# A greedy planner for a four-layer graph network gets a rank and a lead for every kind of operation

## The chip, the core and the metric

The kernel runs on one core of a Trainium2 chip. The metric is the device time of one execution in microseconds (us): the median of several runs. The core has five engines with a queue of instructions each. TensorE (PE) multiplies matrices, and its weight loads (PEld) overlap with its products. VectorE (DVE) and ScalarE (ACT) do elementwise work, GpSimd (POOL) here only the small powers of -0.5, and SyncE (SP) issues all transfers. Each queue is worked off in the order in which the program has written it; semaphores make one engine wait for another.

## The reference

64 graphs of 256 nodes with 256 features pass through four layers in float32. Each layer is `x = layernorm(x + f(x, adj))`:

- Layer 0: four heads; `q`, `k` and `X` are leaky-ReLU projections, `att = sigmoid(q k^T / 8) * adj`, scaled on both sides by the root of the degrees, times `X`, then a layer norm with gain and bias.
- Layer 1: attention with eight heads of 32, masked where `adj` is 0, softmax, times `v`, output projection.
- Layer 2: `adj @ x + eps * x`, a 256 to 1024 projection, RMS norm, SiLU, a 1024 to 256 projection.
- Layer 3: graph attention: `e = leaky(s1_i + s2_j)`, masked softmax, times `x W`, layer norm, exact GELU.

```python
A = dis[..., :, None] * adj_h * dis[..., None, :]          # layer 0
attn = jax.nn.softmax(jnp.where(adj > 0, scores, NEG))     # layer 1, eight heads
h = jax.nn.silu(_rmsnorm(agg @ W1 + b1, rms_weight))       # layer 2
h_prime = jnp.matmul(jax.nn.softmax(e_masked, axis=2), Wh) # layer 3
```

## The kernel before

`weights` describes the loads and small preparations of the constants, and `graph`, called once for each of the 64 graphs, describes the four layers of one graph. Neither issues anything: each call of `op` makes an `Op` with an engine, a planned cost in ns, a function that will issue its instructions, and the values that it reads and writes. A value is a tile of one of six kinds: `s` (128x512, SBUF, 42 slots), `d` (128x1024, 10), `b` (128x2048, 3), `c` (128x32, 72), `p` (a PSUM bank, 8) and `h` (scratch in HBM, 8). The dependencies come from readers and writers.

`Plan.order` then makes the order of all queues by a greedy simulation. It keeps a clock for each engine, and again and again it looks at all operations whose predecessors are placed. For each it works out the earliest start from the engine's clock, the time when its inputs have landed and the time when enough slots are free, and it places the one with the smallest key:

```python
key = start, op.due, op.graph, op.index
```

`due` (lines 149 to 152) runs backwards from the results: it is the least `due` of the successors, held down by the operation's own `turn`. A turn is a number, four to a graph, and stands for one activation table (sigmoid, exp, SiLU, GELU in this order); the turns are opened one after the other (lines 213 to 216), so that ScalarE loads each table once a turn, and at any time several graphs are under way, each in another layer (`ROUND`). Operations without predecessors, which are loads, may be placed when their `due` is within `AHEAD` turns of the open one. `TAIL`, `NEAR` and `ENDS` change a few steps for the first and the last graphs, where a transposition goes over TensorE and not over HBM, or an elementwise step over ScalarE and not VectorE.

TensorE has modes. Most products use the full array. Lines 502 and 582 (scores of layers 0 and 1) run several small products side by side in tiles of rows ("rows"); lines 520, 542, 618 and 680 (degree sums, `A @ X`, attention times `v`, mean of squares) do so in tiles of columns ("columns"). Transposes are a mode of their own. `CHANGE` holds what a switch of mode costs. Because switching costs, the planner adds `STAY` to the start of every TensorE operation of another mode while it is in rows or columns:

```python
if op.engine == "PE" and mode in ("rows", "columns") and mode != op.mode:
    start += STAY - 60 * (op.mode == "transpose")
```

`join` (lines 103 to 143) welds the mean of squares of one graph (line 678) to the first half of layer 1's scores of a graph three further on (line 578), for most graphs; the pair counts as one operation from then on. `emit` sorts the operations by planned start and calls their functions, and that is the order of the instructions in every queue. Slots are given out by the planner too, so waits on buffers follow from the plan.

The names that come up below: line 368 is every product that gives features by tokens (`w_q`, `w_k`), 379 every one that gives tokens by features; 649 is `adj @ x`, 661 the wide projection of layer 2, 707 the narrow one, 722 the projection of layer 3; 323, 625, 693 and 731 are transposes. 470 is the exponential of both softmaxes, 465 the masking in front of it, 697 and 699 the scaling and the SiLU of layer 2, 406, 528 and 688 the powers on GpSimd.

Of the kernel before, what the change touches and what calls it, by code (L numbers as in the profile page):

```python
# [27 lines left out]
DMA_KB, DMA_SEEN = 4, 1900  # L28

WORDS = {"s": 516, "d": 1024, "b": 2048, "c": 32, "p": 512, "h": 1024}  # L30
AHEAD = 12
STAY = 200
NEAR = 1, 2, 3

ENDS = 3
# [3 lines left out]
ROUND = 0, 2, 5, 7  # L39
TAIL = 0, 1, 3, 4  # L40
SLOTS = {"s": 42, "d": 10, "b": 3, "c": 72, "p": 8, "h": 8}


class Value:
# [3 lines left out]
    def __init__(self, kind, name, parts=1):  # L48
        self.kind, self.name = kind, name
        self.writer, self.readers = [None] * parts, [[] for _ in range(parts)]  # L50
        self.uses, self.slot, self.end, self.t = 0, None, 0.0, None
        if kind == "const":
            self.uses, self.slot = 1 << 30, -1
# [29 lines left out]
class Plan:  # L83
# [4 lines left out]
    def __init__(self, graphs):  # L88
        self.graphs = graphs
        self.ops, self.turns = [], {}  # L90
        self.graph = 0

    def op(self, engine, cost, fn, w=(), r=(), turn=None, mode="full", after=None, size=0, joint=None):

        pair = lambda x: (x[0], None if x[0].kind == "p" else x[1]) if isinstance(x, tuple) else (x, None)
        w, r = [pair(x) for x in w], [pair(x) for x in r]
        op = Op(engine, cost, fn, w, r, self.graph, turn, mode, after, size)
        op.table, op.joint, op.leaves = turn is not None and engine == "ACT", joint, mode
        if op.table:
            self.turns[turn] = self.turns.get(turn, 0) + 1  # L100
        self.ops.append(op)

    def join(self):

        joints, before = {}, {}
        for op in self.ops:
            if op.joint is not None:
                joints.setdefault(op.joint[0], []).append(op)
            for nxt in op.after:
                before.setdefault(nxt, []).append(op)  # L110
        gone = set()
        for ops in joints.values():
            if len(ops) == 1:
                continue
            ops.sort(key=lambda op: op.joint[1])
            one, fns = ops[0], [op.fn for op in ops]
            prior = list(dict.fromkeys(p for op in ops for p in before.get(op, ())))
            assert not set(prior) & set(ops)
            for p in prior:
                p.after = list(dict.fromkeys(one if nxt in ops else nxt for nxt in p.after))  # L120
            one.after = list(dict.fromkeys(nxt for op in ops for nxt in op.after))
            for nxt in one.after:
                before[nxt] = list(dict.fromkeys(one if p in ops else p for p in before[nxt]))
                nxt.waits = len(before[nxt])
            before[one], one.waits = prior, len(prior)
            one.fn = lambda fns=fns: [fn() for fn in fns]
            one.cost = sum(op.cost for op in ops) + sum(CHANGE[a.mode, b.mode] for a, b in zip(ops, ops[1:]))
            one.leaves = ops[-1].mode
            one.turn = max((op.turn for op in ops if op.turn is not None), default=None)
            values = [v for op in ops for v in op.values]  # L130
            one.values = list(dict.fromkeys(values))
            for v in one.values:
                v.uses -= values.count(v) - 1
            gone.update(ops[1:])
# [10 lines left out]
    def order(self):  # L145
        for i, op in enumerate(self.ops):
            op.index = i
        self.join()
        for op in reversed(self.ops):
            op.due = min((nxt.due for nxt in op.after), default=4 * (min(op.graph + ROUND[3], self.graphs - 1 + TAIL[3]) + 1))  # L150
            if op.turn is not None:
                op.due = min(op.due, op.turn)
        clock = {e: 0.0 for e in AFTER}
        self.free = {k: [(0.0, i) for i in range(n)] for k, n in SLOTS.items()}
        turns, left = sorted(self.turns), dict(self.turns)
        turn, loaded, mode, moved = 0, None, "full", 0.0
        ready = {op for op in self.ops if not op.waits}
        done = []
        self.busy = {e: 0.0 for e in AFTER}
        while ready:  # L160
            best = None
            for op in ready:
                if (op.due - AHEAD if op.first else op.turn or 0) > turns[turn]:
                    continue
                start = clock[op.engine]
                if op.engine == "PE" and mode in ("rows", "columns") and mode != op.mode:
                    start += STAY - 60 * (op.mode == "transpose")
                start = max(start, op.ready)
                need = {}
                for v in op.values:  # L170
                    if v.slot is None:
                        need[v.kind] = need.get(v.kind, 0) + 1
                for kind, n in need.items():
                    free = self.free[kind]
                    if len(free) < n:
                        break
                    start = max(start, sorted(free)[n - 1][0])
                else:
                    key = start, op.due, op.graph, op.index
                    if best is None or key < best[0]:  # L180
                        best = key, start, op
            if best is None:
                raise RuntimeError(f"the plan is stuck at {len(done)} of {len(self.ops)}")
            _, start, op = best
            op.start = start
            ready.discard(op)
            if op.table and op.turn != loaded:
                op.start, loaded = op.start + TABLE_LOAD, op.turn
            if op.engine == "PE":
                op.start = max(op.start, clock["PE"] + CHANGE.get((mode, op.mode), 0))  # L190
                mode = op.leaves
            end = clock[op.engine] = op.start + op.cost
            op.landed = end + op.seen
            if op.engine == "SP":
                moved = max(moved, end) + op.size * DMA_KB
                op.landed = max(op.landed, moved + DMA_SEEN)
            self.busy[op.engine] += op.cost
            done.append(op)
            op.takes = [v for v in op.values if v.slot is None]
            for v in op.takes:  # L200
                self.free[v.kind].sort()
                v.slot = self.free[v.kind].pop(0)[1]
            for v in op.values:
                v.uses -= 1
                v.end = max(v.end, op.landed)
                if not v.uses:
                    self.free[v.kind].append((v.end, v.slot))
            for nxt in op.after:
                nxt.waits -= 1
                nxt.ready = max(nxt.ready, end + ITSELF[op.engine] if nxt.engine == op.engine != "SP" else op.landed)  # L210
                if not nxt.waits:
                    ready.add(nxt)
            if op.table:
                left[op.turn] -= 1
                while turn < len(turns) - 1 and not left[turns[turn]]:
                    turn += 1
        assert len(done) == len(self.ops)
        self.span = max(op.start + op.cost for op in done)
        return sorted(done, key=lambda op: op.start)
# [533 lines left out]
def gnn_stack_kernel(ctx: ExitStack, tc: tile.TileContext, t: dict, out: bass.AP):  # L753
# [20 lines left out]
        {"space": {"p": bass.MemoryType.PSUM, "h": bass.MemoryType.DRAM}[kind]} if kind in "ph" else {})))  # L774
        for kind in SLOTS}

# [60 lines left out]
```

## Time and profile before

| | |
|---|---|
| median of 3 runs | 2696.62 us (2696.18 to 2699.69) |
| the profiled execution, span | 2698.6 us |
| instructions | 56499 |
| TensorE busy | 2666.0 us, 99% |
| weight loads busy | 2144.9 us, 79% |
| VectorE busy | 2436.7 us, 90% |
| ScalarE busy | 2228.8 us, 83% |
| GpSimd busy | 588.5 us, 22% |
| DMA | 501.01 MB, mean 186 GB/s; the one queue that moves data 67.0% of 16 engines |

The profile is one execution; its span, from the first instruction to the last, is 2.0 us above the median. A busy share is a mean over the whole span. TensorE's products are pipelined and the ends of its instructions are modelled, so the distance from one start to the next says more than the busy time does. In a line of the timeline stand the start, the length in us, the engine, the line of the program, the operation, what is written and read, the shape and the number of instructions; a bracket at the end names what ended an idle time before it. "PE ps L722 <- DVE hT L697: 0.6, 2, 0.4" reads: TensorE at line 722 waited for VectorE's line 697, 0.6 us in all, 2 times, 0.4 at the most.

### The profile page before, as it was taken

What the parts mean: (1) busy time and instruction counts of PE and PEld (TensorE: products, weight loads), DVE (VectorE), ACT (ScalarE), POOL (GpSimd) and SP (SyncE); (2) the same over time, 40 slices, a digit from 0 to 9 for tenths busy, and PEclk for the clock granted to TensorE, in tenths of its full rate; (3) what the DMA queues carried; (4) which work ended last, traced back from release to release, by engine and by line L of the source; (5) the groups of instructions that cost most, each with busy time, mean ns of one, the idle gap of its engine ahead of it and who ended that gap; (6) DMA issues with size and microseconds to landing.
All of it is one profiled execution on the core that took longest, in us unless ns stands there. A gap on an engine that the chain in (4) does not pass through costs nothing.

```text
span 2698.6 us, 56499 instructions
## 1 busy us (share of the span) xinstructions
PE 2666.0 (99%) x17568; PEld 2144.9 (79%) x17568; DVE 2436.7 (90%) x7480; ACT 2228.8 (83%) x5343; POOL 588.5 (22%) x902
## 2 busy tenths in 40 slices
PE   8999999999999999999999999999999999999997
PEld 6777788887887878878888878888788788787776
DVE  6789999999899999999999999989999899999986
ACT  4888888888888988888888888888888888888886
POOL 1111222212222212222222222222222222222212
PEclk9999999999999999999999999999999999999999
DMA  4476875766767767667767677677676676776661
GB/s 146 133 213 176 219 219 161 211 192 183 200 185 187 215 178 189 196 181 207 202 169 206 186 190 212 173 190 201 172 213 193 169 212 189 186 212 181 169 173 36
DMA packets 708045, 501.01 MB, mean 186 GB/s; under 512 B 309792, under 2 KB 667552, under 8 KB 707744
## 3 DMA queue, kind: packets, MB, share of 16 engines
q1 hardware_dynamic: 707744, 497.40, 67.0%
q8 instruction: 140, 2.29, 0.4%
q14 instruction: 161, 1.32, 0.2%
HBM read 301.35 MB, written 195.82 MB: 184 GB/s over the span
## 4 chain that ended last, share of the span: by engine, by line
PE 93%; DVE 3%; ACT 2%; DMA 1%; SPq 1%; issue 1%; POOL 0%; ACTq 0%; POOLq 0%; DVEq 0%
PE ps L368 16%; PE ps L707 16%; PE ps L661 16%; PE ps L379 15%; PE ps L582 5%; PE ps L502 4%; PE ps L542 4%; PE av L618 4%; PE ps L722 4%; PE ps L649 4%; PE ps L323 1%; PE ps L520 1%; PE pr L693 1%; DVE e L465 1%; PE ps L731 0%
## 5 line engine op out<-in xcount | busy, mean ns | idle before, releaser
L470 ACT ACTIVATE e<-e,low 128x256 f32<-128x256 f32 x1152 | 574.6, 500 | 83.7 <-DVE low L465 82.9
L707 PE MATMUL ps<-w,hT 128*128 128x256 f32 x2048 | 466.8, 380 | 1.3 <-ACT hT L699 1.2
L661 PE MATMUL ps<-aggT,w 128*128 128x256 f32 x2048 | 463.4, 380 | 1.6 <-ACT aggT L359 1.0
L707 PEld LDWEIGHTS ps<-w,hT 128*128 128x128 f32 x2048 | 385.7, 190 | 60.4 <-issue 4.6
L661 PEld LDWEIGHTS ps<-aggT,w 128*128 128x128 f32 x2048 | 383.3, 190 | 57.0 <-issue 2.8
L405 POOL TENSOR_SCALAR mv<-mv 128x2 f32<-128x2 f32 x384 | 127.8, 333 | 1316.8 <-DVE mv L395 888.0
L465 DVE CUSTOM_DVE_ANT_0 e<-ps,adj 128x256 f32<-128x256 f32 x1024 | 361.7, 418 | 30.0 <-PE ps L582 29.9
L406 POOL TENSOR_TENSOR mv<-mv,mhalf 128x2 f32<-128x2 f32 x384 | 306.0, 797 | 32.0
L603 DVE STREAM_TRANSPOSE eb<-e 128x1024 f32<-128x1024 f32 x248 | 300.8, 1221 | 0.8 <-ACT e L470 0.7
L668 ACT ACTIVATE hT<-ps,br,r 128x256 f32<-128x256 f32 x512 | 255.7, 585 | 33.9 <-PE ps L707 30.6
L393 DVE BATCH_NORM_STATS2 st<-y 128x6 f32<-128x256 f32 x640 | 238.3, 408 | 1.2
L420 ACT ACTIVATE x<-y,mv 128x256 f32<-128x256 f32 x384 | 215.2, 600 | 28.9 <-DVE mv L416 26.1
L666 ACT ACTIVATE sq<-ps,b 128x256 f32<-128x256 f32 x512 | 220.0, 474 | 20.2 <-PE ps L661 19.7
L470 ACT ACTIVATION_READ_ACCUMULATOR e<-e,low 128x1 f32 x1152 | 219.0, 190 | 0.0
L508 DVE TENSOR_TENSOR att<-att,adjT 128x512 f32<-128x512 f32 x256 | 166.4, 676 | 10.0 <-ACT att L506 10.0
L688 POOL TENSOR_TENSOR rs<-rs,mhalf 128x2 f32<-128x2 f32 x64 | 45.6, 712 | 540.4 <-DVE rs L686 518.9
L528 POOL TENSOR_TENSOR dp<-dp,mhalf 128x8 f32<-128x8 f32 x64 | 110.2, 1722 | 215.8 <-DVE dp L527 168.3
L697 DVE TENSOR_TENSOR hT<-hT,pr 128x1024 f32<-128x1024 f32 x128 | 150.0, 1210 | 5.2 <-PE pr L693 4.3
L582 PE MATMUL ps<-kT,qT 32*128 32x256 f32 x2048 | 146.2, 399 | 0.0
L673 DVE TENSOR_TENSOR sq<-sq 128x512 f32<-128x512 f32 x192 | 129.5, 675 | 11.1 <-ACT sq L666 10.2
L368 PE MATMUL ps<-x0T,w_q 128*128 128x256 f32 x512 | 130.4, 385 | 6.6 <-DMA x0T<-in_xT 6.6
L506 ACT ACTIVATE att<-ps 128x512 f32<-128x512 f32 x256 | 132.2, 603 | 3.8 <-PE ps L502 3.1
(119 smaller groups left out, 5508.9 us busy)
## 6 DMA issues: line engine op xcount, KB each, us to landing
far<-eb SPq DMA_DIRECT2D x248, 512.0 KB, 3.6
eT<-far SPq DMA_DIRECT2D x992, 128.0 KB, 4.1
adj<-in_adj SPq DMA_DIRECT2D x128, 256.0 KB, 5.1
far<-eb SPq DMA_DIRECT2D x488, 64.0 KB, 2.0
x0T<-in_xT SPq DMA_DIRECT2D x64, 256.0 KB, 4.7
adjT<-in_adjT SPq DMA_DIRECT2D x64, 256.0 KB, 4.9
x<-in_x SPq DMA_DIRECT2D x64, 256.0 KB, 5.2
adj<-in_adjT SPq DMA_DIRECT2D x64, 256.0 KB, 4.8
```

Source lines behind the costliest of these rows:

```text
L368: pe.matmul(two(ps)[:, o, :], w.t[:, k, o * P:(o + 1) * P], two(xT)[:, k, :], start=(k == 0), stop=(k == DB - 1))
L379: pe.matmul(two(ps)[:, n, :], two(xT)[:, k, n * P:(n + 1) * P], w()[:, k, :], start=(k == 0), stop=(k == DB - 1))
L393: op("DVE", 328, lambda n=n: dve.bn_stats(st.t[:, 6 * n:6 * n + 6], two(src)[:, n, :]), [(st, n)], [(src, n)])
L406: pool.tensor_tensor(m()[:, :, 2], m()[:, :, 2], c.mhalf[:, :NB], OP.pow)
L465: op("DVE", 345, lambda n=n: dve.tensor_tensor_reduce(out=E(n), in0=two(logits)[:, n, :], in1=two(negmask)[:, n, :], scale=-scale, scalar= ...
L470: op("ACT", 491, lambda n=n: act.activation(E(n), E(n), AF.Exp, bias=low.t[:, n:n + 1], scale=-1.0, accum_out=r.t[:, col(n):col(n) + 1]), ...
L582: pe.matmul(two(pss[i])[:, n, :], two(qT1)[s, hq, n * P:(n + 1) * P], two(kT1)[s, hq, :], start=True, stop=True)
L603: op("DVE", 1155, lambda e=e, eb=eb: dve.transpose(eb.t.rearrange("p (b g i) -> p g b i", b=4, i=32), e.t.rearrange("p (g b i) -> p g b i" ...
L661: pe.matmul(two(ps)[:, i, :], c.w2_1.t[:, k, (j + i) * P:(j + i + 1) * P], two(aggT)[:, k, :], start=(k == 0), stop=(k == DB - 1))
L666: op("ACT", 357, lambda ps=ps, sq=sq, i=i, j=j: act.activation(two(sq)[:, i, :], two(ps)[:, i, :], AF.Square, bias=c.b2_1.t[:, j + i:j + i ...
L668: op("ACT", 491, lambda ps=ps, i=i, j=j: act.activation(Hb(j + i)[:, 0], two(ps)[:, i, :], AF.Identity, bias=c.br2.t[:, j + i:j + i + 1], ...
L707: pe.matmul(two(ps)[:, n, :], Hb(j)[:, 0, n * P:(n + 1) * P], c.w2_2.t[:, j, :], start=(j == 0), stop=(j == HB - 1))
```

## The change

The operations stay as they are, with their costs, values and engines. Every operation gets a kind: the place in the program where it was described, the engine, and its how-manieth it is of these in its graph. All 64 graphs share their kinds; there are 323 in all. `RANK` and `LEAD` hold a number for each kind. `RANK` is added to `due` and `LEAD` (in ns) to the start in the planner's key; the start at which an operation is then placed is the unchanged one. The lead is thus a preference between candidates; the planned start still follows from the clock, the inputs and the slots. Three constants change beside this.

```diff
-AHEAD = 12
-STAY = 200
+AHEAD = 13
+STAY, TURN_STAY = 157, 40
...
+RANK = [
+    0.68, 2.14, 0.01, 0, -0.77, 0.92, -6.01, -4.32, -4.54, -14.31, 2.22, -2.5, 0.34, 0, -4.24, -0.65, -2.92,
...
+LEAD = [
+    0, 0, 0, 0, 33, 209, 0, 98, 689, -8, 30, -381, -441, 197, -191, 0, -61, 0, 3, -17, 0, -27, 457, 0, 15, 37,
...
     def __init__(self, graphs):
         self.graphs = graphs
         self.ops, self.turns = [], {}
+        self.seen = {}
...
         self.ops.append(op)
+        kind = fn.__code__.co_firstlineno, engine
+        n = self.seen.get((self.graph, kind), 0)
+        self.seen[self.graph, kind] = n + 1
+        op.kind = kind, n
...
+        ranks = {}
+        for op in self.ops:
+            op.rank = ranks.setdefault(op.kind, len(ranks))
...
-                    start += STAY - 60 * (op.mode == "transpose")
+                    start += STAY - TURN_STAY * (op.mode == "transpose")
...
-                    key = start, op.due, op.graph, op.index
+                    key = start + LEAD[op.rank], op.due + RANK[op.rank], op.graph, op.index
```

Of the 323 ranks 213 are not zero: 32 of 53 kinds on TensorE, 68 of 107 on VectorE, 47 of 75 on ScalarE, all 8 on GpSimd, 58 of 80 on SP. Of the leads 79 are not zero: 9 on TensorE, 7 on VectorE, 23 on ScalarE, 6 on GpSimd, 34 on SP. The numbers that the prediction names belong to these kinds:

| kind (line of the kernel before) | engine | rank | lead |
|---|---|---|---|
| load of layer 1's `Wo` (238) | SP | -14.31 | -8 |
| load of layer 1's `Wv` (238) | SP | -4.54 | 689 |
| load of `adj`, first of two (313) | SP | 8 | 304 |
| store of the second softmax tile (605) | SP | 0 | 402 |
| third sigmoid of a graph (506) | ACT | -36.53 | 0 |
| first aggregation of the statistics (395) | DVE | -23.02 | 0 |
| transposes of `e`, graphs 0 and 1 (320) | PE | 4.43 and 0 | -384 and -487 |
| `adj @ x`, second half (647) | PE | -7.31 | -475 |
| wide projection, second half of the first pair (659) | PE | -10.72 | -464 |
| wide projection, second half of the last pair (659) | PE | 0 | -1365 |
| mean of squares (678) | PE | -2.81 | 0 |
| power of the RMS norm (688) | POOL | -4.83 | -994 |
| copy of `eT`, last three graphs (357) | ACT | -27.05 | 0 |

## The prediction

> **What bounds the kernel now.** I read the head of the page first, then five stretches of the steady part, then who TensorE waits for there.
>
> ```profile
> span 2698.6 us, 56499 instructions
> PE 2666.0 (99%) x17568; PEld 2144.9 (79%) x17568; DVE 2436.7 (90%) x7480; ACT 2228.8 (83%) x5343; POOL 588.5 (22%) x902
> ```
>
> ```profile
> 800.00:1200.00 400.00, 399.99 (x2654) 322.63 (x2652) 370.21 (x1125) 335.90 (x792) 90.70 (x138) 1.00 0.71 195
> ```
>
> ```profile
> PE ps L722 <- DVE hT L697: 0.6, 2, 0.4
> PE ps L379 <- DVE hT L697: 0.2, 1, 0.2
> ```
>
> The second fence is one of the stretches: TensorE busy 399.99 of 400 us, then weight loads, VectorE, ScalarE, GpSimd, granted clock and DMA share. The two lines of the third are all that TensorE waits for in 400 to 2400 us: 0.8 us. So the bound is TensorE, with VectorE next (370 of 400, some 7% spare). A reordering can't fill gaps there, since there are none; it can only change what is inside the busy time. For that I read the TensorE timeline (start, length, line, count):
>
> ```profile
> 1007.84 1.89 PE L707 MATMUL ps<-w,hT 128*128 128x256 f32 x8
> 1009.66 2.00 PE L502 MATMUL ps<-qT,kT 64*128 64x256 f32 x16
> 1011.58 0.28 PE L625 MATMUL ps<-ident,r 128*16 128x128 f32 x1
> 1011.70 3.62 PE L661 MATMUL ps<-aggT,w 128*128 128x256 f32 x16
> 1015.15 0.38 PE L731 MATMUL ps<-ident,v 128*128 128x128 f32 x2
> ...
> 1030.58 1.95 PE L542 MATMUL ps<-att,v 128*64 128x256 f32 x16
> 1032.46 0.32 PE L680 MATMUL ps<-sq,mean_of 128*32 128x64 f32 x8
> 1032.71 1.15 PE L582 MATMUL ps<-kT,qT 32*128 32x256 f32 x16
> 1033.79 1.99 PE L379 MATMUL ps<-v,eT 128*128 128x256 f32 x8
> 1035.62 1.89 PE L649 MATMUL ps<-adj,x 128*128 128x256 f32 x8
> ```
>
> Starts are what counts. L661's 16 take 1015.15 - 1011.70 = 3.45 us, 0.216 us each: the price of a full-array 256-column instruction. L707's 8, ahead of a row-tiled product, take 1.82 and not 1.73: 0.092 for entering. L502 is eight pairs, 8 x 0.216 = 1.73, and takes 1.92: 0.19 for leaving. L379's 8 after L582 take 1.83: 0.10 more for leaving. A lone excursion into row or column tiles (lines 502, 520, 542, 582, 618, 680) thus costs about 0.39 us over its products. Going over the whole timeline in this way gives 254 excursions (4.0 a graph) and a ledger: 6.6 us before the first matmul, 2541.3 of pure streaming, 115.2 of entering, switching and leaving, 19.7 of waits and slow-clock pitch, and 15.8 from the start of the last matmul to the end. Their sum is 2698.6. All but the streaming, 157 us, is what an order can move.
>
> The rest of the losses lie at the two ends:
>
> ```profile
> 64.50 0.66 PE L323 MATMUL ps<-ident,x 128*128 128x128 f32 x4
> 66.58 3.78 PE L368 MATMUL ps<-xT,w_q 128*128 128x256 f32 x8 [1.42 <-ACT xT L359]
> 70.15 3.08 PE L368 MATMUL ps<-xT,w_k 128*128 128x256 f32 x8
> ...
> 2681.19 1.99 PE L379 MATMUL ps<-v,eT 128*128 128x256 f32 x8 [1.61 <-ACT eT L359]
> ```
>
> In the fill, TensorE waits for ScalarE and then streams 16 instructions in 6.5 us where 3.5 would do: the wait cost more after it than in it. In the drain the last matmuls wait 1.61 us for a transposed softmax, and 15.4 us of work follow them.
>
> **What the Trainium skill says.** "TensorE: Matmul & The Clock Gate", section "What's actually happening": the clock falls to half after an idle window of some 3.4 us, and a busy one brings it back. The trace agrees: 0.41 us an instruction from 66.58 to 73.07, and granted clock 0.92 in 42 to 84 us. "Perfetto Trace Analysis", section "Identifying the Most-Contended Engine": matmul busy share is no measure of distance to the limit. It agrees here: 99% busy hides the 115 us. "ScalarE: Activation LUTs", section "What ACT_TABLE_LOAD costs": about 1283 ns a load, the trace's mean to the nanosecond (L506, L699, L746, L470).
>
> **The change part by part.** No operation, tile, slot count or transfer is added or removed: streaming stays at 2541.3 us, and the 4 table loads a graph stay, since the turns that admit them are untouched. Any order of the same instructions ends no earlier than what precedes, streams and follows.
>
> *RANK* breaks ties. On a saturated engine several operations are ready at the engine's clock, so their first key is equal and `due + RANK` decides. `due` is a whole number, with 4 steps a graph, so -2.8 for the column sums at 678, which carry another graph's first score product with them, lifts the pair by over half a graph, and -10.7 and -7.3 lift second halves (lines 659 and 647) past everything. VectorE and ScalarE are re-sorted in the same way (the third sigmoid by -36.5, the first bn_aggr by -23). On SP 58 of 80 kinds move within the queue; its issue slots and DMA (71% share in the stretch) stay equal in sum. What the sorting can be worth is the excursions: one fewer saves an entry (0.092) and the late part of an exit (0.10), about 0.20 us, since the switch inside a merged run (L542's 1.88 against 1.73) costs about what the first part of an exit does. Bounds: at best one fewer a graph, 64 x 0.20 = 13 us gained; at worst one more in every second graph, 6 us lost. I take 40 fewer, 8 us. This is a choice: runs of three already occur (line 1030.58 ff.), lone ones are still over half, and the second halves kept together free PSUM slots sooner, which lets the next tiled product be ready beside another.
>
> *LEAD* shifts the compared start. Only four steady kinds on TensorE have it. The -475, -464 and -1365 belong to second halves whose operands are those of the first halves and whose PSUM slot is already held, so they could start anyway: no idle is bought, cost 0, hidden by TensorE's own stream. Without that cover, -1365 could buy 1.4 us a graph, 87 us. GpSimd's -994 on L688 reserves its queue for the pow of the RMS norm. Behind it stand the layer-norm pows (L405 with L406, 1.1 us), and behind these VectorE L416 and ScalarE L420; GpSimd is 22% busy, so the cover is its own idle time. SP's +402 and +304 let other issues pass one 512 KB store of a softmax tile and a mask load. Its four readers on SP and L618 stand behind it; loads take 4 to 5 us to land and lie a fraction of a graph (42 us) ahead, cost 0 while that holds.
>
> *STAY 200 to 157, TURN_STAY 60 to 40* make leaving cheaper in the planner: a full operation now beats a tiled one that comes ready 157 to 200 ns later. The measured cost of leaving and coming back is 0.39, less a switch of 0.15 to 0.2. So 43 ns of window decide few cases; bounds -2 to +4 us, taken as 0. *AHEAD 13* admits first loads one turn, a quarter of a graph, earlier; cost 0, hidden by the SP queue.
>
> *The ends.* Kinds that exist only in graphs 0, 1 and 61 to 63, or are weights, have their own numbers: w1_o -14.3 in rank, w1_v +689, transposes of e -384 and -487, the last graphs' eT copy -27. In the first 90 us some 9 of the 19.7 us are lost, half of it at the slow pitch that follows one 4 us episode of waits; I take 4 back (bounds 0 to 7). In the drain there are 5.7 us of waits after 2584 us and the 15.4 us tail; I take 4 back (bounds -3 to 8), because VectorE works on three graphs at once there and the last one's chain only has to go first.
>
> Sum: 8 + 4 + 4 = 16 us, 2698.6 - 16 = 2682.6 in the profiled execution. That execution stands 2.0 us above the median of the runs (2696.62), so the forecast for the median is 2680.6 us.
>
> **Rivals.** *Ends only:* the excursions stay near 254, and 8 us come back at both ends: 2689. For it: greedy ties are as likely to break a run as to make one, and STAY points that way. Against it: 32 of 53 TensorE kinds are re-ranked. *No visible change:* a gain at one end is given back as excursions, 2692 to 2702. For it: steady TensorE is already without waits. Against it: too many decisions move for the sum to be just nil. *Slower, lost cover before L707:* L707 begins at a median of 0.9 us after the Silu of its first half (L699), least 0.05, by the timeline of the two. The new ranks put VectorE's scaling L697 or the Silu behind other work. If that makes TensorE wait 0.35 us a graph, 64 x 0.35 = 22 us against the gain of 16: 2703. It decides from 0.25 us a graph. For it: VectorE at 93% catches up slowly. Against: the planner only places L707 when its operand has landed by its own costs, and those fit (0.432 a pair of instructions, as measured; 92 ns entry, as measured), so it would fill the gap with another graph's products.
>
> **How the numbers follow.** Forecast 0.50, ends only 0.25, no visible change 0.10, slower 0.15. A difference of 0.2% (5.4 us) is about what a measurement here can tell from none: faster 0.75, same 0.10, slower 0.15. Best sum: 13 + 2 + 7 + 8 = 30, 2667, and a little below if steady waits shrink too; worst taken in: half of the slower case. Range 2662 to 2702. The forecast's own case with its bounds spans 2667 to 2687.
>
> **What would show it.** Excursions counted on the TensorE timeline: near 215 (right), 254 or more (wrong). First full-clock stretch: whether the 66 us episode is gone. The tail after the last matmul: under 15.4. TensorE waits in 400 to 2400 us: still under 2 us, else the slower rival. Wrong altogether: if waits on VectorE or DMA appear in the steady part, or if the granted clock dips there.

## The result and the profile after

The changed kernel takes 2686.96 us (median of 4 runs, 2686.04 to 2687.04) against 2697.22 us before (4 runs, 2696.18 to 2699.69): a ratio of 0.9954, 95% interval 0.9940 to 0.9969. A second measurement gave 2686.76 against 2698.16 us, ratio 0.9955 (0.9942 to 0.9967). So it is faster by 10 to 11 us between the medians and by 12 us, or 0.45%, by the ratios. In the kernel after, every line from 368 on stands 42 lines further down: 410 is the former 368, 421 is 379, 703 is 661, 749 is 707, 764 is 722.

The head of its page, and one of the steady stretches (columns as before):

```profile
span 2685.1 us, 56560 instructions
PE 2658.0 (99%) x17568; PEld 2141.2 (80%) x17568; DVE 2433.4 (91%) x7480; ACT 2241.1 (83%) x5343; POOL 564.8 (21%) x902
```

```profile
800.00:1200.00 400.00, 400.00 (x2676) 322.55 (x2676) 369.00 (x1141) 337.10 (x808) 85.62 (x136) 1.00 0.71 191
```

The steady stretch looks the same as before: TensorE full, VectorE at 369 of 400 us. What TensorE waits for in 400 to 2400 us is still under 1 us (0.8 before, 0.9 now):

```profile
PE ps L764 <- DVE low L507: 0.5, 2, 0.3
PE ps L421 <- ACT hT L710: 0.2, 1, 0.2
PE ps L764 <- issue: 0.2, 1, 0.2
```

The difference is in the fill. TensorE's timeline of the kernel after, over the stretch in which the kernel before waited at 62 to 67 us and then ran 16 instructions in 6.5 us:

```profile
56.49 1.04 PE L365 MATMUL ps<-ident,e 128*128 128x128 f32 x8
57.36 1.89 PE L421 MATMUL ps<-w_l,x0T 128*128 128x256 f32 x8
59.09 1.04 PE L365 MATMUL ps<-ident,e 128*128 128x128 f32 x8
59.96 1.89 PE L421 MATMUL ps<-w_l,x0T 128*128 128x256 f32 x8
61.69 1.03 PE L321 MATMUL ps<-w_o,b_v 128*128 128x256 f32 x4
62.55 1.24 PE L365 MATMUL ps<-ident,e 128*128 128x128 f32 x8
...
67.93 1.89 PE L410 MATMUL ps<-xT,w_q 128*128 128x256 f32 x8
69.66 1.89 PE L410 MATMUL ps<-xT,w_k 128*128 128x256 f32 x8
```

The transposes of graph 0's softmax, which have to wait for ScalarE's exponentials one after the other, now have the projections of later graphs between them, where before those had been done ahead and 16 transposes stood together. Nothing waits there, and the two projections at 67.93 and 69.66 take 0.216 us an instruction.

The first matmul also begins earlier. Before and after, in the list of waits of TensorE:

```profile
PE ps L368 <- DMA x0T<-in_xT: 6.6, 1, 6.6
```

```profile
PE ps L410 <- DMA w_q<-in_L_gnn_W_q: 4.5, 1, 4.5
```

Counting every start-to-start distance on the TensorE timeline gives the same ledger as in the prediction, here by place (us). "Fill" is the first 320 us of streaming, "end" the last 321; "in and out" is what entering, switching and leaving tiled modes cost; "waits" includes the slow-clock pitch. A wait that ends at a switch of mode counts as "in and out"; in these four executions such waits come to 1 to 2 us. The two columns on the right are experiments that follow.

| | before | after | fill_only | end_only |
|---|---|---|---|---|
| to the first matmul | 6.6 | 4.5 | 4.4 | 6.3 |
| fill: in and out / waits | 20.8 / 9.2 | 20.0 / 2.4 | 19.8 / 3.4 | 19.9 / 9.8 |
| middle: in and out / waits | 80.8 / 2.1 | 80.3 / 2.1 | 81.0 / 5.6 | 81.1 / 3.1 |
| end: in and out / waits | 13.6 / 8.4 | 12.3 / 5.0 | 13.2 / 8.1 | 12.3 / 4.4 |
| after the last matmul | 15.4 | 17.0 | 15.6 | 17.2 |
| streaming | 2541.3 | 2541.3 | 2541.3 | 2541.3 |
| excursions | 254 | 246 | 254 | 251 |
| span | 2698.6 | 2685.1 | 2692.6 | 2695.8 |

Of the 13.5 us between the two profiled executions the fill makes 9.7, the middle 0.5 and the end 3.1. The forecast had expected half of its gain from fewer excursions; there are 8 fewer, not 40, and none of these 8 is in the fill: 5 are in the middle and 3 at the end.

### The profile page after: what moved, and what is told of

It is laid out like the page before. It is cut to its first block, busy times and chain, and to the rows that moved or that the text cites. A ratio compares the mean times of both kernels' runs of the same rounds, so it can differ in the third digit from the quotient of the medians.

```text
span 2685.1 us, 56560 instructions
## 1 busy us (share of the span) xinstructions
PE 2658.0 (99%) x17568; PEld 2141.2 (80%) x17568; DVE 2433.4 (91%) x7480; ACT 2241.1 (83%) x5343; POOL 564.8 (21%) x902
## 4 chain that ended last, share of the span: by engine, by line
PE 91%; DVE 4%; ACT 1%; SPq 1%; DMA 1%; issue 1%; POOL 0%; ACTq 0%; DVEq 0%; POOLq 0%
PE ps L410 16%; PE ps L749 16%; PE ps L703 15%; PE ps L421 15%; PE ps L624 5%; PE ps L544 4%; PE ps L584 4%; PE av L660 4%; PE ps L764 4%; PE ps L691 4%; PE ps L365 1%; PE ps L562 1%; PE pr L735 1%; DVE e L507 1%; DVE st L435 1%
## 5 line engine op out<-in xcount | busy, mean ns | idle before, releaser
L703 PE MATMUL ps<-aggT,w 128*128 128x256 f32 x2048 | 466.4, 381 | 1.4 <-DVE low L507 1.4
L703 PEld LDWEIGHTS ps<-aggT,w 128*128 128x128 f32 x2048 | 381.7, 190 | 61.8 <-issue 7.6
L447 POOL TENSOR_SCALAR mv<-mv 128x2 f32<-128x2 f32 x384 | 111.7, 291 | 1254.9 <-DVE mv L437 772.7
L448 POOL TENSOR_TENSOR mv<-mv,mhalf 128x2 f32<-128x2 f32 x384 | 300.6, 783 | 32.0
L708 ACT ACTIVATE sq<-ps,b 128x256 f32<-128x256 f32 x512 | 220.4, 470 | 19.8 <-PE ps L703 19.4
L550 DVE TENSOR_TENSOR att<-att,adjT 128x512 f32<-128x512 f32 x256 | 165.6, 680 | 15.4 <-ACT att L548 15.1
```

The costliest lines, as they stand in the source:

```text
L448: pool.tensor_tensor(m()[:, :, 2], m()[:, :, 2], c.mhalf[:, :NB], OP.pow)
L703: pe.matmul(two(ps)[:, i, :], c.w2_1.t[:, k, (j + i) * P:(j + i + 1) * P], two(aggT)[:, k, :], start=(k == 0), stop=(k == DB - 1))
L708: op("ACT", 357, lambda ps=ps, sq=sq, i=i, j=j: act.activation(two(sq)[:, i, :], two(ps)[:, i, :], AF.Square, bias=c.b2_1.t[:, j + i:j + i ...
```

## The experiments

The theory after the traces: **ends**, the gain is in the fill and to a smaller part in the end. Its rivals: **sum**, the prediction's own steps, in which each part of the change has its small worth and excursions carry half; and **fit**, that the tables and constants only work together, because each placement moves all later ones.

### The parts alone

The new constants alone:

```diff
-AHEAD = 12
-STAY = 200
+AHEAD = 13
+STAY, TURN_STAY = 157, 40
...
-                    start += STAY - 60 * (op.mode == "transpose")
+                    start += STAY - TURN_STAY * (op.mode == "transpose")
```

> AHEAD 13, STAY 157, TURN_STAY 40 without the tables. The step of the prediction: -2 to +4 us, so 2695 to 2701, as the parts add up. The rival, that tables and constants are one fit and each part alone breaks the regular runs: the written order has 292 excursions and not 254; if only entering and leaving is paid, 38 x 0.2 to 0.45 = 8 to 17 us more, 2705 to 2714; if VectorE and the buffers fall out of step too, TensorE waits and it is 2730 to 2750.

Measured: 2757.86 us, ratio 1.0218 (1.0200 to 1.0237), which is 58 us slower.

RANK alone, on the kernel after:

```diff
-AHEAD = 13
-STAY, TURN_STAY = 157, 40
+AHEAD = 12
+STAY, TURN_STAY = 200, 60
...
-                    key = start + LEAD[op.rank], op.due + RANK[op.rank], op.graph, op.index
+                    key = start, op.due + RANK[op.rank], op.graph, op.index
```

> RANK alone, with LEAD zero and the old constants. The step of the prediction: 40 fewer excursions, 8 us, and some of the ends: 2682 to 2690. The rival of one fit: the written order has 341 excursions; by entering and leaving alone 87 x 0.2 to 0.45 = 17 to 39 us more, 2714 to 2736; with TensorE waiting as well, 2770 to 2795.

Measured: 2786.71 us, ratio 1.0325 (1.0306 to 1.0344), 87 us slower.

LEAD alone, with the old constants as in rank_only:

```diff
-                    key = start + LEAD[op.rank], op.due + RANK[op.rank], op.graph, op.index
+                    key = start + LEAD[op.rank], op.due, op.graph, op.index
```

> LEAD alone, with RANK zero and the old constants. The step of the prediction: 0, apart from the ends: 2690 to 2697. The rival of one fit: the written order has 309 excursions; by entering and leaving alone 55 x 0.2 to 0.45 = 11 to 25 us more, 2708 to 2722; with waits as well, 2735 to 2755.

Measured: 2764.34 us, ratio 1.0242 (1.0224 to 1.0261), 65 us slower.

All three (two runs each) fall where "fit" had put them or a little above, far outside "sum". The waits of TensorE over the whole execution show the kind of loss; of const_only, two of the costliest:

```profile
PE ps L707 <- ACT hT L699: 8.6, 5, 3.7
...
PE ps L707 <- ACT v L726: 6.7, 3, 3.2
```

and of rank_only (its lines stand as in the kernel after, so 741 is the SiLU and 730 the pow of the RMS norm):

```profile
PE ps L749 <- ACT hT L741: 12.8, 12, 2.0
PE ps L722 <- DVE sq L717: 7.9, 3, 3.4
PE pr L735 <- POOL rs L730: 5.2, 6, 2.5
```

Many are waits on the long chain of layer 2 (statistics, pow, scaling, SiLU), up to 3.7 us at a time, of which the kernels before and after have almost none in the middle. Added up over the execution, without the wait for the first transfers, the waits that the profile lists, those over 0.15 us, come to 44 us in const_only, 57 in rank_only and 42 in lead_only, and to 10 in the kernel before. So of the 53, 85 and 63 us by which these profiled executions are longer, 34, 47 and 32 are waits. The excursions are 292, 341 and 309, which is 38, 87 and 55 more; at the price found in the next section that is some 9, 20 and 13 us, and what remains, 10 to 18 us, is slow clock and shorter waits, which were not told apart. All of it comes from one part of a set of numbers without the others. No part has a worth of its own that could be added. The tables together without the constants, and one table with the constants, were not run.

### What one excursion costs

The prediction had priced an excursion more at 0.20 us. This kernel is the one before, with 56 merged runs cut by a single exchange of neighbours on TensorE:

```diff
-    for op in plan.order():
+    for op in split(plan.order()):
...
+    for last, op, nxt in zip(pe, pe[1:], pe[2:]):
+        if not (side(last.leaves) and side(op.mode) and not side(nxt.mode)):
+            continue
...
+        done.insert(j, done.pop(i))
```

> The kernel before with 56 merged runs of tiled products cut in two, by moving one operation behind the TensorE operation that follows it, where nothing in between reads or replaces what it holds. 310 excursions and not 254, all else in its order. By the prediction's price of 0.20 us for one excursion more, 11 us slower; by what the parts run alone show (0.45 to 0.60 us for each added one), 25 to 34 us slower, if that price belongs to the excursion and not to the disorder around it.

Measured: 2718.40 us, ratio 1.0072 (1.0056 to 1.0087): 20.2 us by the medians, 0.36 us for each of 56. But not all of this is the price of an excursion. What was moved back comes one operation later, and in the fill and at the end TensorE then waits more. Two waits in split; the kernel before has none in the place of the first and 0.35 us in that of the second:

```profile
107.08 1.10 PE L661 MATMUL ps<-aggT,w 128*128 128x256 f32 x4 [1.69 <-issue]
189.92 2.03 PE L661 MATMUL ps<-aggT,w 128*128 128x256 f32 x4 [1.92 <-ACT aggT L359]
```

The waits over 0.15 us come to 17.4 us, against 10.3 before. The middle is free of this: there TensorE waits 0.2 us in split and 0.6 before, 37 of the 56 cuts lie in it, and it takes 8.4 us longer, which is 0.23 us for each. Both expectations missed the whole: the price of 0.20 was near, and its 11 us were exceeded by the waits; the 0.45 to 0.60 of the parts alone was not borne out. Where a tiled operation has been cut off, both sides of it can be read:

```profile
1010.28 1.93 PE L618 MATMUL av<-eT,v 128*32 128x256 f32 x32
1012.14 1.99 PE L707 MATMUL ps<-w,hT 128*128 128x256 f32 x8
1013.97 1.89 PE L649 MATMUL ps<-adj,x 128*128 128x256 f32 x8
```

L618 streams 8 x 0.216 = 1.73 us and takes 1.86 to the next start, 0.13 for leaving; L707's eight take 1.83, 0.10 over their 1.73. The entry is 0.09. A switch from columns to columns, in the kernel after (L660 and L584 are the former L618 and L542):

```profile
1012.59 1.93 PE L660 MATMUL av<-eT,v 128*32 128x256 f32 x32
1014.45 1.95 PE L584 MATMUL ps<-att,v 128*64 128x256 f32 x16
```

It takes 1014.45 - 1012.59 = 1.86 and so costs the first part and none of the other two. Merging thus saves the 0.10 and the 0.09, about 0.19, which agrees with the 0.23 of the middle.

### Where the gain is

The tables and constants are on for a part of the turns only; otherwise ranks and leads are zero and the constants old:

```diff
-            best = None
+            best, on = None, turns[turn] < 4
...
-                    key = start + LEAD[op.rank], op.due + RANK[op.rank], op.graph, op.index
+                    key = start + on * LEAD[op.rank], op.due + on * RANK[op.rank], op.graph, op.index
```

(`AHEAD`, `STAY` and `TURN_STAY` are pairs indexed by `on` in the same way.) With `< 4` only the loads ahead of the first matmuls change:

> The tables and the new constants hold only while the first turn is open, which in the written order changes nothing but the loads ahead of the first matmuls: the two query and key weights go out before the features. 254 excursions as before. If the time before the first matmul is worth what the two traces show (6.57 against 4.47 us), the kernel is 2 us faster than before, 2695, and its trace still has the waits at 62 to 67 us and the slow pitch behind them. If the fill is no cause of the gain, because TensorE has slack to make up later, no change: 2697. If the 66 us episode hangs on these loads too, 9 us faster, 2688.

Measured: 2696.53 us, ratio 0.9990 (0.9981 to 0.9998). The first matmul starts at 4.32 us and not 6.57. The gain of 2.7 us, with an interval from 0.5 to 5, is what this start predicts.

With `< 240`, all but the end:

> Tables and new constants until turn 240 is opened (some 94% of the graphs), then ranks and leads of zero and the old constants. The written order has 249 excursions. If the gain lies in the fill, as the two ledgers say (9 of 13.5 us), 7 to 10 us faster than before: 2687 to 2690, with the fill of the kernel after. If the last turns carry it, no gain: 2695 to 2698.

Measured: 2694.59 us, ratio 0.9983 (0.9976 to 0.9989), a gain of 4.6 us and thus under the expectation. Its profile says why: the fill is that of the kernel after, but soon after the switch to zero ranks TensorE waits 4.2 us in five pieces between 2570 and 2582 us, where before waits 0.7, and runs at half clock for the 3.4 us from 2577 on. That the zero ranks fall out of step with what they take over is the likely reason.

```profile
2577.00 2.21 PE L691 MATMUL ps<-adj,x 128*128 128x256 f32 x4 [2.29 <-ACT x L462]
```

So this run separates nothing; the hand-over is an effect of its own. With `>= 220`, the end alone:

> The kernel before until turn 220 is opened, and tables and new constants from there on. The written order has 251 excursions. If the gain lies in the fill, at most 4 us: 2693 to 2697, with the waits at 62 to 67 us still there. If the end carries it, 8 to 12 us: 2685 to 2689.

Measured: 2695.48 us, ratio 0.9989 (0.9981 to 0.9997), a gain of 3.0 us. Its waits at 62 to 67 us are those of before. The last one came from a switch at which the written order returns to 254 excursions and to the end of before, `< 52`:

> Tables and new constants until turn 52 is opened (the first fifth of the graphs), then ranks and leads of zero and the old constants. In the written order the excursions return to the regular pattern of before: 254, as before, and the end is that of before. It has the new fill and nothing else. If the fill carries the gain, as the two ledgers say (6.6 us for what every execution loses there, up to 3 more where the clock falls): 6 to 9 us faster than before, ratio 0.9967 to 0.9978, and fill and end_only (3 us) together make some nine of the twelve us. If the steady part carries it: ratio 0.999 or more, as first_turn.

Measured: 2691.53 us against 2699.49, ratio 0.9972 (0.9961 to 0.9982), a gain of 7.6 us (4.9 to 10.5). Its TensorE timeline is the fill of the kernel after, line by line:

```profile
57.31 1.89 PE L421 MATMUL ps<-w_l,x0T 128*128 128x256 f32 x8
59.04 1.04 PE L365 MATMUL ps<-ident,e 128*128 128x128 f32 x8
```

Its 3.5 us more of waits in the middle are mainly one wait of 1.9 us at 620 us with half clock behind it; the same wait took 0.36 us in before, 1.36 in end_only and 1.07 in first_turn, so it differs from one execution to the next.

Fill and end together: 0.9972 x 0.9989 = 0.9961, and the whole change has 0.9954 or 0.9955. Some 1.6 to 1.9 us are left for the middle, where 5 fewer excursions at 0.23 would be 1.2 and the ledger finds 0.5. The intervals are wider than this remainder, so whether the middle gained is not shown; that the fill carries the largest part is shown.

### Does the slow clock cost 3 us

The kernel before with eight more matmuls in the waits of the fill, to keep TensorE occupied:

```diff
             def fn(o=o):
+                for _ in range(WARM if b == 1 and w is c.w1_q and not o else 0):
+                    pe.matmul(two(ps)[:, o, :], c.ident, c.w0_q.t[:, 0, :], start=True, stop=True)
                 for k in range(DB):
...
         def fn():
+            for _ in range(warm):
+                pe.matmul(dst()[:, 0, :], c.ident, c.w0_q.t[:, 0, :], start=True, stop=True)
```

`WARM` is 4, and `warm` is 2 for two of the transposes of e of graph 0. The results of the added products are overwritten by what follows them.

> The kernel before with eight extra matmuls of constants (each two instructions of 0.216 us, 3.5 us in all) put where TensorE waits between 62 and 67 us: two before each of two transposes of e of graph 0 and four before the query projection of graph 1. Nothing is left out and the order is the same. If the waits' idleness drops the clock and so doubles the pitch of the next 16 instructions, these stream in 3.5 us and not 6.5, while the extra work overhangs the waits by some 0.5 us: 2 to 3 us faster, 2694 to 2695, with the granted clock 1.00 in 42 to 84 us. If the slow pitch has another cause, 0.5 us slower: 2698.

Measured: 2697.68 us, ratio 0.9997 (0.9989 to 1.0005), no difference that the runs can tell (3.0 us faster to 1.3 slower). Its trace does what the theory said; the two projections after the waits:

```profile
66.32 1.89 PE L373 MATMUL ps<-xT,w_q 128*128 128x256 f32 x8
68.04 1.89 PE L373 MATMUL ps<-xT,w_k 128*128 128x256 f32 x8
```

16 instructions in 3.45 us, not 6.5. From the first transpose of e to the end of these the kernel before takes 11.7 us and this one 9.1. The answer to the riddle is in split, which has the waits of before unchanged:

```profile
65.97 0.65 PE L323 MATMUL ps<-ident,x 128*128 128x128 f32 x4
68.05 1.99 PE L368 MATMUL ps<-xT,w_q 128*128 128x256 f32 x8 [1.43 <-ACT xT L359]
69.88 1.89 PE L368 MATMUL ps<-xT,w_k 128*128 128x256 f32 x8
```

The same waits, and no slow pitch behind them: 8.8 us over the stretch. Of the 16 instructions 14 are slow in before and in end_only, 7 in first_turn, none in split. The granted clock shows it directly: it is 0.50 for 6.8 us in before (from 65.7 us on) and in end_only, for 3.4 us in first_turn. The fall of the clock after these waits is thus a matter of the single execution, 0 to 3 us, which fits what the Trainium skill says in "TensorE: Matmul & The Clock Gate", section "What's actually happening": the activity window runs freely and isn't reset by the kernel. Against an execution that stays at full clock the warm matmuls are 0.3 us slower (9.1 against 8.8), so they can win only in those where the clock falls.

How often that is can be read from the runs, since each has the mean granted clock of its span. Half clock for 6.8 us takes 0.0013 from it, so the third decimal tells. Of 86 runs of the kernel before on four chips, 39 have 0.998 and 47 have 0.997 or 0.996, and on each chip the latter take 2.2 to 3.8 us longer in the mean. With the warm matmuls 12 of 13 runs have 0.998. This points to a clock that falls somewhere in about half of the executions, and to warm matmuls that prevent it in nearly all: half of 3 us less 0.3 is an estimate of 1.2 us, and between the medians of before and warm there are 1.5. In which place the clock fell is known of the profiled executions alone.

First loads and warm matmuls together:

> The kernel before with two things of the new fill only: the loads ahead of the first matmul as in first_turn (2.2 us in its trace) and the eight extra matmuls in the waits at 62 to 67 us as in warm (2.6 us in its trace after the extra work). 254 excursions, the steady part and the end as before. If the fill losses carry through to the end, as they must where TensorE never waits again, 4 to 5 us faster than before. If warm's 0.0003 was right and its trace an exception, 2 us.

Measured: 2695.59 us, ratio 0.9991 (0.9983 to 1.0000), 2.4 us: nearer to the second branch, though the interval (0 to 4.6) reaches the first. Again 12 of 13 runs have a clock of 0.998. What fill_only's 7.6 us have beyond this would be the waits themselves (2.4 us), in whose place fill_only does work that is needed anyway, and cheaper switches (1.0 by the ledger); this was not tried by itself.

### Is there more in the tables

The same program with other numbers, and the kernel after once more beside it:

```diff
-STAY, TURN_STAY = 157, 40
+STAY, TURN_STAY = 132, 14
...
 RANK = [
...
 LEAD = [
...
```

> The same program with other numbers in RANK and LEAD (291 and 164 of 323 differ), STAY 132 and TURN_STAY 14, found by letting the numbers drift while the planner's last clock falls. 239 excursions in the written order, 7 fewer than the kernel after. If a better fit of the plan carries to the chip, 2 to 5 us faster than the kernel after, 0.1 to 0.2%; if the plan is already closer than the chip follows it, no change or up to 3 us slower.

Measured: 2685.74 us (2683.37 to 2688.43), ratio 0.9955 (0.9942 to 0.9967). The kernel after, beside it on the same chip:

> The changed kernel unaltered, beside the others on one chip. By the first measurement 10 us under the kernel before, ratio 0.995 to 0.997.

Measured: 2686.76 us, ratio 0.9955. No difference. By the ledger refit saves 4.3 us of in and out (106.5 against 110.9 in the profile of the kernel after that was taken beside it) and loses it again: 3.2 us more waits and slow pitch, and a first matmul at 6.3 us and not 4.3, where it waits for `w_k`:

```profile
6.30 3.75 PE L430 MATMUL ps<-x0T,w_k 128*128 128x256 f32 x8 [6.30 <-DMA w_k<-in_L_gnn_W_k]
```

The planner's own last clock, which is there without the chip, is 2687.6 us for the kernel before and 2676.5 for the one after, 11.1 less. For const_only, rank_only and lead_only it is 2736.2, 2779.8 and 2736.8, for refit 2672.6. So it has the sign and about the size of every large difference above, but not refit's 4 us: what the planner's clocks don't know, when the first transfers really land and when TensorE's clock falls, is as large here as what they can still gain.

## Why the prediction was right, and where it was not

The time was right: 2680.6 us forecast, range 2662 to 2702, measured 2686.96; a gain of 16 was foretold and 10 to 12 were there. That it came so near is in part luck: half of the 16 was put on excursions that did not go away, and the two ends gave more than they were given. Point by point:

- **The bound, the constancy of the streaming, the ledger**: right. 2541.3 us in both kernels; TensorE without waits in the middle of both; all gain came from the 157 us around the streaming.
- **RANK, "I take 40 fewer, 8 us"**: wrong, and this is the step that failed. There are 8 fewer, 5 in the middle and 3 at the end; by the ledger in and out falls by 0.5 us in the middle and by 1.3 at the end, together what 8 excursions at 0.23 would be. The price of 0.20 was about right (0.23 in the middle of split); the number of excursions was not. The grounds given, that lone excursions were over half and that kept pairs free slots, said that room was there and not that this set of numbers would use it. The parts run alone point the other way: each of them costs 38 to 87 excursions, so that 254 was already a good state for this planner, and the whole change ends close to it.
- **STAY and AHEAD, "bounds -2 to +4, taken as 0"** and **LEAD, "cost 0"**: wrong as worths of parts. Alone they cost 58 and 65 us. The working looked at what one decision costs where it is taken and left out that every later placement follows from it. In the whole change this doesn't show, since the numbers were fitted together. The claim that the -1365 buys no idle on TensorE was not tried by itself; the profile after has no waits at the second halves of L703 in the middle, which agrees with it.
- **The fill, "I take 4 back (bounds 0 to 7)"**: the right place and too small. 7.6 us by fill_only, 2.2 of it the first matmul, which the prediction had put under what precedes the streaming and had given nothing.
- **The end, "I take 4 back (bounds -3 to 8)"**: 3.0 us by end_only, so about right in sum. But the tail, which was to be under 15.4 us, is 17.0: waits and in and out give 4.7 back, and the work after the last matmul takes 1.6 of it. VectorE has more left to do then: it is busy for 11.7 us of the 17.0, and was for 9.7 of the 15.4 before.
- **The rivals**: "ends only" named the mechanism, with 8 us where the ends give 10.6. It also came nearer in its number: 2689 against the likeliest case's 2680.6, with 2686.96 measured. "Lost cover before L707" did not happen in the whole change, but it is what rank_only shows (12.8 us on that very pair), so the mechanism was real and the price of 22 us of the right order for it.
- **The clock, "The trace agrees"**: in the halving, yes (0.43 us and not 0.216, 14 of the 16 instructions). An idle stretch of some 3.4 us, which is quoted there, is not in the trace: the longest wait ahead of the slow pitch is 1.42 us, the three together 2.4.
- **The sum "with its bounds spans 2667 to 2687"**: the upper end does not follow from the bounds given. Their worst values are 6, 4, 0 and 3 us lost, which is 2710.

## What to carry to other kernels

In a greedy plan on a saturated engine, the parts of a fitted set of numbers can't be priced one by one: each alone was 2 to 3% slower and the whole 0.45% faster. When the saturated part of a kernel has no waits left, look at the fill first: put independent full-size products between operations that wait on a slow partner, and issue what the first product waits for ahead of everything else. To price fewer mode switches, cut some on purpose and measure, but take the price from a stretch in which the cuts bring no new waits: here 0.23 us, close to the 0.20 from reading one stretch, while the whole execution gave 0.36. And where a plan is simulated before it is emitted, read its clock before pricing its parts by hand.

## What the runs showed of the hardware

The same 2.4 us of idle in three pieces between transposes was followed by 14, 14, 7 and 0 instructions at 0.43 us and not 0.216 in the profiled executions of before, end_only, first_turn and split. A single profile therefore over- or understates such a fill by up to 3 us, as much as a fourth of the whole gain here.

In the profiles of all kernels here the granted clock falls to half 23 times between the first 15 us and the last fall, which lasts to the end, and it stays there for 3.41 us (13 times) or 6.83 us (10 times), for no other length. It needs no idle stretch as long as that: a single wait of 1.88 us (fill_only, 620 us) or 1.92 us (split, 190 us) went before a fall.

The times of the kernel before spread over 8 us (2694.4 to 2702.6 in 17 runs on one chip), those of the kernel after over 3 (2684.1 to 2687.2 in 5). In the 17 runs the 8 with a granted clock of 0.998 took 2696.7 us in the mean and the other 9 took 2700.0, so the clock makes a good part of the spread; the kernel after has too few runs to say whether it escapes it for this reason.
